# Two transformer layers on one core: transposes at the ends of attention units moved to VectorE in 32x32 blocks, the rotary pair exchange done by a shuffle, and an RMS norm applied behind its products

## The chip, the cores and the metric

The kernel runs on one core of a Trainium2 chip. The metric is the device time of one execution in microseconds (us). The core has five engines that run their own instruction queues in order: PE (TensorE; the profile lists its weight loads apart, as PEld), DVE (VectorE), ACT (ScalarE), POOL (GpSimd) and SP (SyncE, which here only issues DMAs). They wait for each other through semaphores. PE writes its products to PSUM, eight banks of 128 partitions by 512 fp32 numbers; everything else lies in SBUF (128 partitions) or in HBM, the chip's main memory.

## The reference, cut to what matters

The input is 4096 rows of 256 features. Two layers follow each other, both with a layer norm first and a residual sum behind, and all attentions have 16 heads of width 16:

```python
xn = layernorm(x)
x  = x + sparse_attention(xn) + fp8_product(xn)          # layer 0
xn = layernorm(x)
x  = x + rope_attention(xn) + moe_block(xn)              # layer 1

def sparse_attention(x):     # keys: every 8th row, and the query's own block of 128, masked
    q, k, v = split(x @ W + b); return softmax(q k^T / 4 + mask) v @ Wproj + bproj
def rope_attention(x):       # full causal attention
    q, k, v = split(x @ Wqkv)
    rope(t) = t * cos + (-t_odd, t_even interleaved) * sin        # pairs of features
    return softmax(rope(q) rope(k)^T / 4 + causal) v @ Wproj
def moe_block(x):
    h = rms(x) * n1_w        # rms(x) = x * rsqrt(mean(x*x) + EPS)
    q = rms_per_head(h @ wq.T) * qn_w;  k = rms_per_head(h @ wk.T) * kn_w;  v = h @ wv.T
    x = x + softmax(q k^T / 4 + causal) v @ wo.T                   # first 64 columns zeroed
    xf = rms(x) * n2_w
    return x + weighted sum of the best two of four experts(xf)   # first 64 columns zeroed
```

So there are three attentions: a = 0 (sparse), a = 1 (rotary) and a = 2 (inside the MoE block, full causal).

## The kernel before

**Tiling.** Rows are cut into 8 chunks of 512 (CW), each of four tiles of 128 (P); heads into 4 groups of four. One **unit** (`unit`, line 1194) is one attention `a`, one group `g` and one chunk `ch` of queries: 3 x 4 x 8 = 96 units. A causal unit of chunk ch has 4(ch+1) tiles of 128 keys, a sparse one has four tiles of strided keys and the local blocks. I call the work on one such tile of keys a **round**: scores of four heads (`st_a`), their exponentials on ACT (`pt_a`), and the products with the values into one PSUM bank (`po_a`).

**Two passes over the scores.** The softmax subtracts the true maximum. The first pass (`causal_max`, `strided_max`, `local_max`, from line 947) makes scores with queries along the partitions in `pm_a` (`pms_a`, `pml_a`) and DVE reduces each 512-wide bank to a column of `mx_a`. The second pass (`exponentials`, line 1021) makes them again the other way round, adds the negated maximum by a small product with the constant `pick` and the tile `sh_a`, and exponentiates. The first pass of one unit runs interleaved with the second pass of the unit in front, one group of maxima with each half round.

**Between the passes of a unit.** `reduced` (line 990) takes the maximum over a unit's columns (`nm_a`), splits it in a high and a low part, and lays the two in `pad`. `shift` (line 1004) transposes the four tiles of `pad` on PE into a bank (`ps_a`), and ACT copies the bank to `sh_a`, where the 16 rows that are needed lie along the queries.

**At the end of a unit.** `out_copied` (line 1099) copies the sums out of PSUM (`oc_a`), `out_turned` (line 1103) transposes them on PE in four blocks of 128x128 (`pot_a`), `out_divided` (line 1108) copies that bank (`od_a`, ACT), inverts the softmax sums (`rd_a`, DVE), and multiplies (`on_a`, POOL). When the four groups of a chunk are done, two further sets of four PE transposes (`pon`, by `turn`, line 266) turn the result back, ACT copies it (`ot`, `proj_copied`, line 1123), and `projected` and `added` (lines 1128, 1162) make the output projection and the residual sum.

**Preparation.** `prepare0` (line 393) and `prepare1` (line 484) make q, k and v of one chunk for layer 0 and for layer 1 and store them in HBM. In `prepare1`, q and k of the rotary attention are each made twice, with the weights and with the weights whose columns are swapped in pairs (`_swap`, line 1368), so that rope is two multiplications on DVE and one addition on POOL. For the MoE attention the layer-normed rows are multiplied by their RMS factor (`scaled`, line 514: `hr`), transposed once more on PE (`pth`) and scaled by n1_w on the way out (`kept_h`, line 521: `ht`).

**Order.** `Schedule` (line 65) sorts all pieces by a key; one unit of key is about four rounds. A unit starts its second pass at a0 and its first pass at m0 = a0 - lag. `units` (line 1276) sets the lag: at least size + 0.5, where size is ch + 1 for a causal unit and 1.25 for a sparse one. For causal units of chunks 1 to 7 the lag is size + 1; for the first 20 units it is size + 0.5. `between` (line 1282) puts a **block** of preparation and expert work, all at one key, into the gap behind certain units; there are nine. `add_ring` and `add_open` hold back pieces that need a PSUM bank: four banks in the ring "bank" (scores of the second pass, transposes, projections), three in the ring "max" (first pass, experts). The helper `InOrder` (line 42) keeps every engine to the order in which the pieces come; since it records each instruction, nearly all groups of the profile carry its line, L52, and are told apart by tile names.

**Queues.** Almost all DMAs go through SP in that same order: key tiles for both passes (`load_k`, line 862, keys m0 - 1 + i and a0 - 1 + i), values, queries, weights, and the stores. SP waits until a DMA's buffer is free, and everything behind it waits too.

Of the kernel before, what the change touches and what calls it, by code (L numbers as in the profile page):

```python
# [37 lines left out]
RMS_EPS = 1.1920929e-07  # L38
F32_MAX = 3.4028234663852886e38
# [69 lines left out]
def tile_two_layers(ctx: ExitStack, tc, d, out):  # L109
# [44 lines left out]
    y_d = dram.tile([NCH, P, TPC, E], BF16, name="y_d")  # L154
    x1_d, xn_d, s_d, x2_d, xs_d = (
# [6 lines left out]
    with ExitStack() as at:  # L162
# [23 lines left out]
        pads = []  # L186
        for i in range(2):
            pad = c1.tile([P, TPC, 2, 64], F32, name=f"pad{i}")
            nc.gpsimd.memset(pad, 0.0)
            nc.gpsimd.memset(pad[:, :, :, 2 * HPG : 2 * HPG + 1], 1.0)  # L190
            pads.append(pad)
# [109 lines left out]
        def act_piece(todo, fn):  # L301
            todo.append((fn, None, None))
# [49 lines left out]
        def v_products(todo, src, w, a, place, bias, nm):  # L352

            for tp in range(2):
# [11 lines left out]
                def drain(z=z, tp=tp):  # L366
                    v = vst[vst_no[0] % 2]
                    vst_no[0] += 1
                    act.copy(
                        v.rearrange("p t h d -> p (t h) d")[:, :, 0:D], z["p"].rearrange("p t (h d) -> p (t h) d", d=D)  # L370
                    )
# [112 lines left out]
        def prepare1(ch):  # L484
# [4 lines left out]
                [("w1", 2), ("w1", 3), ("w1", 0), ("w1", 1), ("w1", 4), ("w2", 1), ("w2", 2), ("w2", 0)], nm,  # L489
# [17 lines left out]
            def squares():  # L507
                sp.dma_start(xn_d[ch], s["x"])
                s["rr"] = rms(s["x"], nm)
# [4 lines left out]
            def scaled():  # L514
                s["hr"] = work.tile([P, TPC, E], F32, tag="t1", name="hr" + nm)
                for t in range(TPC):
                    dve.tensor_scalar(s["hr"][:, t, :], s["x"][:, t, :], s["rr"][:, t : t + 1], None, ALU.mult)

            act_piece(todo, scaled)

            def kept_h(f, pt):
                if f == 0:
                    s["ht"] = work.tile([P, 2, CW], F32, tag="ht", name="ht" + nm)
                act.activation(s["ht"][:, f, :], pt, AF.Copy, scale=nw1[:, f : f + 1])


            for n, (what, dst) in enumerate((("k", k_d[1]), ("q", q_d[1]))):
# [3 lines left out]
                def part(half, i, n=n, what=what, scale=scale, parts=parts):  # L531
                    z, name = parts[half], f"{what}1{half}"

                    def mm():
                        feature_product(z, w[2 * n + i], s["xt"], half, f"p{name}{i}{nm}")

                    def ev():
                        z[i] = work.tile([P, CW], F32, tag=f"r{i}", name=f"r{i}_{name}{nm}", bufs=2 - i)
                        dve.scalar_tensor_tensor(z[i], z["p"], scale, s["cs"][:, i, :], ALU.mult, ALU.mult)
                        if i:  # L540
                            pool.tensor_tensor(z[0], z[0], z[1], ALU.add)

                    todo.append((mm, "bank", ev))

                for i in range(2):
                    for half in range(2):
                        part(half, i)
                    act_piece(todo, w.fetch)
# [7 lines left out]
                if n == 0:  # L556
                    turn(todo, lambda: s["hr"], kept_h, "pth" + nm)

            v_products(todo, lambda: s["xt"], lambda: w[4], 1, ch, None, nm)


            for what, n, wcol, dst in (("k", 5, 1, k_d[2]), ("q", 7, 0, q_d[2])):
# [13 lines left out]
                def sq2(tp, z=z, name=name):  # L576
                    if tp == 0:
                        z["raw"] = work.tile([P, TPC, E], F32, tag="t1", name=f"raw_{name}{nm}")
                        z["ss"] = small.tile([P, TPC * H], F32, tag="ss2", name=f"ss2_{name}{nm}")
                        z["rs"] = small.tile([P, TPC * H], F32, tag="rs2", name=f"rs2_{name}{nm}")  # L580
                    act.copy(z["raw"][:, 2 * tp : 2 * tp + 2], z[tp])
                    sq = work.tile([P, 2 * E], F32, tag="r1", name=f"sq2_{name}{tp}{nm}")
# [4 lines left out]
                def norms2(z=z, name=name):  # L587

                    x, y = z["ss"], z["rs"]
                    t = small.tile([P, TPC * H], F32, tag="nt2", name=f"nt2_{name}{nm}")  # L590
                    dve.tensor_scalar(x, x, 1.0 / D, RMS_EPS, ALU.mult, ALU.add)
# [30 lines left out]
            v_products(rest, lambda: s["ht"], lambda: w[6], 2, ch, None, nm)  # L622
# [8 lines left out]
        def rms(x, nm):  # L631

            sq = work.tile([P, CW], F32, tag="r1", name="sqj" + nm)[:, :E]
# [3 lines left out]
            ve = small.tile([P, TPC], F32, tag="ve", name="rve" + nm)  # L637
            dve.tensor_scalar(ve, ss, 1.0 / E, RMS_EPS, ALU.mult, ALU.add)
            rs = small.tile([P, TPC], F32, tag="rr", name="rrs" + nm)
            pool.tensor_tensor(rs, ve, mhalf[:, :TPC], ALU.pow)  # L640
            return rs
# [39 lines left out]
        def experts(ch):  # L681
# [7 lines left out]
            def squares():  # L689
                s["rr"] = rms(s["x"], nm)  # L690
# [299 lines left out]
        def reduced(u, n):  # L990

            neg = small.tile([P, TPC * HPG], F32, tag="nm", name="nm_" + u["nm"])
# [3 lines left out]
            pad = pads[unit_no[0] % 2]  # L996
            unit_no[0] += 1
            src = neg.rearrange("p (t h) -> p t h", h=HPG).unsqueeze(2).to_broadcast([P, TPC, 2, HPG])
            high = pad[:, :, :, 0 : 2 * HPG : 2]
            dve.tensor_copy(pad.bitcast(F32R)[:, :, :, 0 : 2 * HPG : 2], src)  # L1000
            dve.tensor_tensor(pad[:, :, :, 1 : 2 * HPG : 2], src, high, ALU.subtract)
            u["pad"] = pad.rearrange("p t i c -> p t (i c)")

        def shift(u):
            ps_ = bank_tile("ps_" + u["nm"])
            for t in range(TPC):
                pe.transpose(ps_[:, tt(t)], u["pad"][:, t], ident)
            u["sh"] = work.tile([P, CW], F32R, tag="sh", name="sh_" + u["nm"], bufs=2)
            act.copy(u["sh"], ps_)
# [87 lines left out]
        ons, proj = {}, {}  # L1097
# [5 lines left out]
        def out_turned(u):  # L1103
            u["pt"] = bank_tile("pot_" + u["nm"])
            for t in range(TPC):
                pe.transpose(u["pt"][:, tt(t)], u["oc"][:, tt(t)], ident)

        def out_divided(u):
            od = work.tile([P, CW], F32, tag="oc", name="od_" + u["nm"], bufs=2)
            act.copy(od, u["pt"])  # L1110
            v = od.rearrange("p (q r) -> p q r", r=R)
            rd = small.tile([P, TPC * HPG], F32, tag="rd", name="rd_" + u["nm"])
            dve.reciprocal(rd, v[:, :, D])
            at_ = u["a"], u["ch"]
            if u["g"] == 0:
                ons[at_] = work.tile([P, TPC, E], F32, tag="on", name=f"on_{u['nm']}", bufs=2)
            on = ons[at_].rearrange("p t (g h d) -> p t g h d", g=G, d=D)[:, :, u["g"]]
            pool.tensor_tensor(
                on, v[:, :, 0:D].rearrange("p (t h) d -> p t h d", h=HPG),
                rd.rearrange("p (t h) -> p t h", h=HPG).unsqueeze(3).to_broadcast([P, TPC, HPG, D]), ALU.mult,  # L1120
            )

        def proj_copied(a, ch, f, pt):
            if f == 0:
                proj["ot"] = work.tile([P, 2, CW], F32, tag="xt", name=f"ot_{a}_{ch}")
            act.copy(proj["ot"][:, f, :], pt)

        def projected(a, ch, tp):
            n = wp[a].shape[2]
            pp = bank_tile(f"pp_{a}_{ch}_{tp}").rearrange("p (t f) -> p t f", t=2)  # L1130
            for j in range(2):
                for c in range(2):
                    pe.matmul(
                        pp[:, j, :n], proj["ot"][:, c, tt(2 * tp + j)], wp[a][:, c, :],
# [59 lines left out]
        def unit(a, g, ch, a0, lag, m0, own_at):  # L1194
# [8 lines left out]
            for kc in keys:  # L1203
                at = tiles.index((kc, 0)) / TPC if a and kc != ch else own_at / TPC if a else keys.index(kc)
                sched.add(m0 - 1.0 + at, load_k, u, kc, "km")
# [279 lines left out]
```

## Time and profile before

| what | value |
|---|---|
| median of 3 runs | 5221.17 us (5215.86 to 5225.06) |
| the profiled execution | 5228.83 us, of which the profile's span is 5227.1 us |
| PE busy | 5021.6 us, 96% of the span |
| DVE busy | 3636.3 us, 70% |
| ACT busy | 3163.8 us, 61% |
| POOL busy | 577.6 us, 11% |
| mean granted TensorE clock | 0.977 of full speed |
| DMA | 737.31 MB, 141 GB/s on average |

The profile's page gives busy times for the whole span. It is read here together with four answers of the trace: groups of instructions with their shapes (number, busy time in us, mean ns of one, idle time in front of them), tables of windows (busy time of each engine in one stretch of time, with the number of instructions in brackets), the timeline, and the list of DMAs with the time from issue to landing. Transposes count one record each on PE; an fp32 product of 128 rows of contraction counts two. The busy time of a group is the union of its records, which overlap, so it is less than number times mean.

### The profile page before, as it was taken

The page shows a single profiled execution, that of the slowest core. Times are in us where ns is not written, and L with a number is a line of the kernel's source. Part 1 is how long each engine was busy: PE and PEld are TensorE (multiplying, and loading weights), DVE is VectorE, ACT ScalarE, POOL GpSimd, SP SyncE. Part 2 cuts the span into 40 slices and gives each one's busy share as a digit, 9 for nine tenths or more (in the row PEclk, how much of TensorE's full clock was granted, in tenths as well). Part 3 has the DMA queues.
Part 4 walks back from the last instruction along what each step waited for, and adds up shares of the span by engine and source line. Part 5 has one row for each costly group of instructions (what it writes and reads, how often), then busy time and mean ns, then how long its engine had stood idle before and what let it go on. Part 6 is the DMA issues. An engine that isn't in the chain of part 4 may idle for free.

```text
span 5227.1 us, 98240 instructions
## 1 busy us (share of the span) xinstructions
PE 5021.6 (96%) x35680; PEld 2674.8 (51%) x35680; DVE 3636.3 (70%) x8215; ACT 3163.8 (61%) x6351; POOL 577.6 (11%) x557
## 2 busy tenths in 40 slices
PE   6788899999999999999999999999999999999999
PEld 3455555555655555554545454545445544444445
DVE  4655774777488838888387886588885698888701
ACT  2544573576367736777376775567774567777752
POOL 3232113111201020100301001001001000000000
PEclk7889899999999999999999999999999999999999
DMA  5465545444634444433544334434334433333222
GB/s 192 148 209 183 172 150 184 157 158 136 203 119 152 142 153 158 149 123 130 172 144 145 121 120 140 154 118 140 119 106 146 152 113 127 113 118 119 98 76 80
DMA packets 497458, 737.31 MB, mean 141 GB/s; under 512 B 97104, under 2 KB 203088, under 8 KB 496976
## 3 DMA queue, kind: packets, MB, share of 16 engines
q1 hardware_dynamic: 492576, 728.58, 42.1%
q8 instruction: 285, 4.67, 0.4%
q10 hardware_dynamic: 4400, 2.45, 0.2%
q14 instruction: 197, 1.61, 0.1%
HBM read 586.90 MB, written 143.95 MB: 140 GB/s over the span
## 4 chain that ended last, share of the span: by engine, by line
PE 84%; DVE 7%; issue 4%; POOL 2%; DMA 1%; ACT 1%; SPq 0%; ACTq 0%; POOLq 0%; DVEq 0%
PE st_a L52 27%; PE po_a L52 22%; PE pm_a L52 12%; DVE pms_a L52 2%; PE pe_m L52 2%; PE pk L52 2%; PE pq L52 2%; PE pp L52 2%; DVE mx_a L52 1%; PE pml_a L52 1%; PE pv L52 1%; PE pms_a L52 1%; PE ps_a L52 1%; PE pot_a L52 1%; POOL x L52 1%
## 5 line engine op out<-in xcount | busy, mean ns | idle before, releaser
L52 ACT ACTIVATE pt_a<-st_a 128x512 f32<-128x512 f32 (+3 forms) x5248 | 2599.9, 572 | 1056.6 <-PE st_a L52 1002.7
L52 DVE TENSOR_REDUCE mx_a<-pm_a 128x1 f32<-128x512 f32 x3584 | 2232.0, 683 | 301.1 <-PE pm_a L52 225.8
L52 PE MATMUL pm_a<-km_a,q_a 64*128 64x512 f32 (+3 forms) x4608 | 1840.4, 434 | 21.3 <-DVE mx_a L52 18.4
L52 PE MATMUL st_a<-q_a,ke_a 64*128 64x512 f32 (+3 forms) x5632 | 1777.3, 401 | 1.7 <-ACT pt_a L52 1.6
L52 PE MATMUL st_a<-sh_a,pick_r 64*128 64x512 f32 (+3 forms) x5248 | 1729.5, 398 | 0.0
L52 PEld LDWEIGHTS st_a<-q_a,ke_a 64*128 64x128 f32 x5632 | 899.6, 187 | 1022.2 <-ACT pt_a L52 919.4
L52 PE MATMUL po_a<-pt_a,v 128*32 128x512 f32 (+3 forms) x11264 | 1325.0, 549 | 0.0
L52 PEld LDWEIGHTS pm_a<-km_a,q_a 64*128 64x128 f32 x4608 | 843.2, 185 | 360.2 <-DVE mx_a L52 313.4
L52 PEld LDWEIGHTS st_a<-sh_a,pick_r 64*128 64x128 f32 x5248 | 951.5, 187 | 44.0 <-issue 2.9
L52 DVE CUSTOM_DVE_ANT_0 pm_a<-pm_a,never_sb 128x512 f32<-128x512 f32 (+3 forms) x1024 | 482.2, 515 | 182.3 <-PE st_a L52 97.0
L52 DVE CUSTOM_DVE_ANT_0 pms_a<-pms_a,hidden_sb 128x512 f32<-128x512 f32 x512 | 341.0, 719 | 85.0 <-PE pms_a L52 77.2
L52 POOL TENSOR_TENSOR on_a<-od_a,rd_a 128x256 f32<-128x256 f32 x96 | 59.6, 621 | 3064.1 <-DVE rd_a L52 3064.1
L52 PEld LDWEIGHTS po_a<-pt_a,v 128*32 128x32 f32 x11264 | 228.6, 108 | 306.8 <-issue 273.6
L52 PE MATMUL pms_a<-km_a,q_a 64*128 64x512 f32 x512 | 224.3, 509 | 33.4 <-DVE mx_a L52 18.5
L52 PE MATMUL st_a<-mcol_sb,identb_sb 64*128 64x128 bf16 x2048 | 255.2, 224 | 0.0
L52 DVE SCALAR_TENSOR_TENSOR acc_m<-pe_m,g_wt_m,acc_m 128x192 f32<-128x192 f32 x128 | 52.6, 416 | 268.9 <-PE pe_m L52 268.9
L52 DVE DVE_READ_ACCUMULATOR2_ANT mx_a<- 128x1 f32 x1536 | 217.8, 142 | 0.0
L52 PEld LDWEIGHTS pms_a<-km_a,q_a 64*128 64x128 f32 x512 | 95.7, 195 | 67.1 <-DVE mx_a L52 49.8
L52 PEld LDWEIGHTS <-identb_sb 64*128 64x128 bf16 x2048 | 114.0, 96 | 12.0 <-issue 4.1
L52 ACT CAST sh_a<-ps_a 128x512 fp32r<-128x512 f32 x96 | 56.2, 586 | 91.9 <-PE ps_a L52 91.9
L52 DVE TENSOR_REDUCE mx_a<-pml_a 128x4 f32<-128x512 f32 x128 | 83.1, 688 | 25.5 <-PE pml_a L52 25.3
L52 POOL TENSOR_TENSOR xa<-xa,pa 128x512 f32<-128x512 f32 (+1 forms) x48 | 56.9, 1185 | 357.4 <-ACT pa L52 350.6
(401 smaller groups left out, 4167.4 us busy)
## 6 DMA issues: line engine op xcount, KB each, us to landing
km_a<-k_d SPq DMA_DIRECT2D x704, 256.0 KB, 4.1
ke_a<-k_d SPq DMA_DIRECT2D x704, 256.0 KB, 3.1
k_d<-hl_k SPq DMA_DIRECT2D x100, 512.0 KB, 3.3
q_d<-hl_q SPq DMA_DIRECT2D x96, 512.0 KB, 4.8
q_a<-q_d SPq DMA_DIRECT2D x192, 256.0 KB, 4.6
v<-v_d SPq DMA_DIRECT2D x352, 136.0 KB, 4.0
w<-in_w_dram SPq DMA_DIRECT2D x85, 256.0 KB, 4.7
w_l<-in_l_dram SPq DMA_DIRECT2D x80, 256.0 KB, 2.9
```

The costliest lines, as they stand in the source:

```text
L52: got = emit(*args, **kw)
```

## The change

1. **The maxima.** `reduced` packs the high and low parts into 32 columns, transposes them on DVE in 32x32 blocks (`turned`, tile `tu`), and SP writes the blocks with four DMAs to a new tensor `shift_d` in HBM. `shift` is now two DMAs on SP that read the unit's 8 rows back, twice, into one of two standing tiles (`rows_`) whose row of ones was laid out at the start. PE transposes `ps_a` and the ACT copy are gone. Both steps get new keys: a0 - lag + size + 0.05 and + 0.1 (before: a0 - min(0.8, lag - size - 0.05), and a0 - min(0.3, lag - size - 0.3)).
2. **The outputs.** `out_turned` is gone; `out_divided` transposes `oc` on DVE (512 columns, 32x32 blocks), inverts on DVE and multiplies on POOL into a tile `om` that two groups share; behind every second group `out_returned` transposes `om` back on DVE into `ot`. The four `pon` sets and their ACT copies are gone. The rows of the projection weights are reordered on the host to suit (`_by_turns`).
3. **Rope.** The products with swapped weights are gone. ACT copies the product out of PSUM, DVE exchanges neighbours by a stream shuffle, POOL multiplies by sin, DVE multiplies by cos, POOL adds.
4. **The MoE norm.** `hr` and `pth` are gone: `ht` is `xt` times n1_w, made on ACT. The RMS factor is applied where v leaves PSUM (two ACT instructions of 256 columns in place of one of 512), and for q and k it is folded into the EPS term of the norm per head (`norms2`: one small DVE instruction more).
5. **Smaller.** The load of a sparse unit's own keys for the first pass goes from key m0 to m0 + 0.4. Some tiles change tags and buffer counts.

```diff
-            pad = pads[unit_no[0] % 2]
+            pad = small.tile([P, TPC, HPG, 2], F32, tag="pad", name="pad_" + u["nm"])
+            src = neg.rearrange("p (t h) -> p t h", h=HPG)
+            high = pad[:, :, :, 0]
+            dve.tensor_copy(pad.bitcast(F32R)[:, :, :, 0], src)
+            dve.tensor_tensor(pad.bitcast(F32R)[:, :, :, 1], src, high, ALU.subtract)
+            turned = small.tile([P, R], F32, tag="tu", name="tu_" + u["nm"])
+            dve.transpose(turned, pad.rearrange("p t h i -> p (t h i)"))
+            no = unit_no[0]
             unit_no[0] += 1
...
+            rows = shift_d[no].rearrange("r (t b j) -> b t r j", t=TPC, b=TPC)
+            for b in range(TPC):
+                sp.dma_start(rows[b], turned[R * b : R * (b + 1), :])
+            u["no"], u["sh"] = no, rows_[no % 2]

         def shift(u):
-            ps_ = bank_tile("ps_" + u["nm"])
-            for t in range(TPC):
-                pe.transpose(ps_[:, tt(t)], u["pad"][:, t], ident)
-            u["sh"] = work.tile([P, CW], F32R, tag="sh", name="sh_" + u["nm"], bufs=2)
-            act.copy(u["sh"], ps_)
+            for half in (0, 64):
+                sp.dma_start(u["sh"].bitcast(F32)[half : half + 2 * HPG, :], shift_d[u["no"]])
...
         def out_divided(u):
             od = work.tile([P, CW], F32, tag="oc", name="od_" + u["nm"], bufs=2)
-            act.copy(od, u["pt"])
+            dve.transpose(od, u["oc"])
...
+        def out_returned(u):
...
+            dve.transpose(proj["ot", at_][:, f, :], outs.pop(at_))
...
                     def ev():
-                        z[i] = work.tile([P, CW], F32, tag=f"r{i}", name=f"r{i}_{name}{nm}", bufs=2 - i)
-                        dve.scalar_tensor_tensor(z[i], z["p"], scale, s["cs"][:, i, :], ALU.mult, ALU.mult)
-                        if i:
-                            pool.tensor_tensor(z[0], z[0], z[1], ALU.add)
+                        z[0] = work.tile([P, CW], F32, tag="r0", name=f"r0_{name}{nm}", bufs=2)
+                        act.activation(z[0], z["p"], AF.Copy, scale=scale)
+
+                    def rotated():
+                        z[1] = work.tile([P, CW], F32, tag="r1", name=f"r1_{name}{nm}", bufs=2)
+                        dve.stream_shuffle(z[1], z[0], PAIRS)
+                        pool.tensor_tensor(z[1], z[1], s["cs"][:, 1, :], ALU.mult)
+                        dve.tensor_tensor(z[0], z[0], s["cs"][:, 0, :], ALU.mult)
+                        pool.tensor_tensor(z[0], z[0], z[1], ALU.add)
...
-            sched.add(a0 - min(0.8, lag - size - 0.05), reduced, u, len(keys))
-            sched.add_ring(a0 - min(0.3, lag - size - 0.3), "bank", 1, shift, u)
+            sched.add(a0 - lag + size + 0.05, reduced, u, len(keys))
+            sched.add(a0 - lag + size + 0.1, shift, u)
...
-            put(e0 + 0.12, lambda: out_turned(u), "bank", lambda: out_divided(u))
+            sched.add(e0 + 0.05, out_divided, u)
+            if g % 2:
+                sched.add(e0 + 0.35, out_returned, u)
             if g == G - 1:
-                turns = []
-                turn(turns, lambda: ons[a, ch], lambda f, pt: proj_copied(a, ch, f, pt), f"pon_{a}_{ch}")
-                for f in range(2):
-                    put(e0 + 0.5 + 0.13 * f, *turns[f])
```

## The prediction

> **What bounds the kernel now.** I read the page first: busy times and the chain of waits.
>
> ```profile
> PE 5021.6 (96%) x35680; PEld 2674.8 (51%) x35680; DVE 3636.3 (70%) x8215; ACT 3163.8 (61%) x6351; POOL 577.6 (11%) x557
> ...
> PE 84%; DVE 7%; issue 4%; POOL 2%; DMA 1%; ACT 1%; SPq 0%; ACTq 0%; POOLq 0%; DVEq 0%
> ```
>
> PE looks like the only bound, and the change takes PE work away. The groups by shape give its size (busy us, mean ns of one):
>
> ```profile
> L52 PE MATMUL pk<-xt,w 128*128 128x512 f32 x184 | 91.7, 628 | 2.3 <-ACT xt L52 2.3
> L52 PE MATMUL pq<-xt,w 128*128 128x512 f32 x184 | 85.3, 593 | 0.0
> ...
> L52 PE MATMUL ps_a<-ident_sb,pad 128*128 128x128 f32 x384 | 64.8, 293 | 2.1 <-DVE pad L52 2.1
> ...
> L52 PE MATMUL pot_a<-ident_sb,oc_a 128*128 128x128 f32 x384 | 63.0, 287 | 0.0
> ...
> L52 PE MATMUL pon<-ident_sb,on_a 128*128 128x128 f32 x192 | 31.2, 285 | 1.0 <-ACT pt_a L52 0.8
> ...
> L52 PE MATMUL pth<-ident_sb,hr 128*128 128x128 f32 x64 | 10.2, 283 | 0.0
> ```
>
> Rope's second products are 2 halves x 2 contractions x 2 records = 8 records of pk and 8 of pq per chunk, 64 of each in all: 64 x 91.7/184 + 64 x 85.3/184 = 61.6 us. With the four transposes PE loses 64.8 + 63.0 + 31.2 + 10.2 + 61.6 = 230.8 us. But an average over the span hides what else is full, so I cut single rounds out of a unit of chunk 5 (windows; PE, PEld, DVE, ACT, POOL busy):
>
> ```profile
> 3416.69:3419.45 2.76, 2.76 (x46) 1.87 (x45) 2.49 (x5) 2.65 (x6) 0.00 (x0) 1.00 0.56 195
> 3419.45:3422.83 3.38, 3.38 (x27) 1.56 (x25) 2.60 (x5) 2.71 (x7) 0.00 (x0) 1.00 0.00 0
> 3422.83:3425.57 2.74, 2.74 (x23) 1.23 (x21) 2.57 (x5) 1.93 (x5) 0.62 (x1) 1.00 0.00 1
> 3425.57:3428.30 2.73, 2.73 (x23) 1.21 (x21) 2.48 (x5) 2.07 (x5) 0.00 (x0) 1.00 0.82 267
> ```
>
> The last row is a plain full round: 2.73 us, in which DVE's four reductions take 2.48. DVE is 91% busy here, not 70%. The second row holds `pot`: 0.65 us longer. The third holds the reciprocal (0.25 us of DVE) and is no longer: it fits in DVE's 0.25 us of idle time. The timeline shows why nothing more would fit. In each round PE waits about 0.3 us for DVE to free a bank of the first pass, with three such banks for pairs of products. So **PE and DVE are locked together**, and DVE work above 0.25 us in a round delays PE by the excess.
>
> **Part 1, preparation blocks.** Per chunk go 7.5 us of rope products (16 records at some 0.47 us, the pace inside these windows) and 1.2 us of `pth`. Two of the blocks:
>
> ```profile
> 252.00:343.00 91.00, 59.99 (x238) 38.42 (x228) 42.76 (x100) 28.61 (x56) 43.44 (x37) 0.79 0.56 184
> ...
> 1833.00:1978.00 145.00, 140.25 (x528) 85.93 (x528) 55.10 (x138) 48.50 (x89) 43.90 (x37) 0.98 0.52 170
> ```
>
> The second has an expert body and PE is full (97%); six chunks are prepared in such blocks: 6 x 8.7 = 52 us gained. DVE and POOL have room there for a shuffle, a multiplication (taken at the 0.69 us of the `r_k` row, against two of these removed) and one more POOL multiplication of 1.27 us (row `r_k<-r_k,r_k`). In the first kind PE is busy 60 of 91 us and waits 15.4 us for `raw_q` from DVE; with POOL at 43 us and 5 us more, I count 6 us for those two blocks (bounds -10 and +17). `norms2` gets a DVE instruction of 0.19 us on the path PE waits for, 16 times: 3 us lost. **Sum: 55 us gained.**
>
> **Part 2, transposes on DVE.** No row shows a DVE transpose. Nearest is the reduction of 128x512 (0.62 us from start to start, 0.68 for one): below, it can't be cheaper than about 0.6, as it passes the same 512 elements. Above, fp32 might go at half or a quarter of that pace: 1.2 or 2.3 us. [...] For 32 columns I take the 0.19 us of `pad`.
>
> In a full round with `pot`, the new time is the larger of PE's and DVE's: 3.38 - 0.65 = 2.73, against 2.48 + 0.69 + 0.25 = 3.42. **So moving the output transpose gains nothing there**: its 0.65 us come back as 0.68. The transpose back (every second unit) adds 2.48 + 0.69 - 2.73 = 0.44 in the next round. I made this comparison for every round outside the blocks, with its own length and DVE time. `ps` sits in rounds on the diagonal, whose score products are narrower, and gives nearly all its 0.65: -64 us with those that also hold `pon`. The 32-column transpose costs +9, the output transposes +2 (gains in chunk 0 and at the end, losses elsewhere), `pon` against the way back 0. **Sum: 53 us gained of 154 removed**; at 0.62 us it would be 61, at 1.2 us a loss of 11, at 2.3 us a loss of 155.
>
> [...] With DVE simply full, each added instruction would cost its whole time: 96 x (0.19 + 0.69) + 48 x 0.69 = 118 us against 154, a gain of 36. The rows give more, as a round has 0.25 us free and not all rounds are full.
>
> ACT loses the `sh`, `od` and `ot` copies (56 + 57 + 29 us) and gains 32 of 0.6. It is never the last here; I count nothing.
>
> **Part 3, the maxima through HBM.** This is a new wait. Before, in the timeline of an early unit (start, length, engine):
>
> ```profile
> 568.99 0.19 DVE L52 TENSOR_REDUCE nm_a<-mx_a 128x16 f32<-128x32 f32 x1
> ...
> 570.88 0.66 PE L52 MATMUL ps_a<-ident_sb,pad 128*128 128x128 f32 x4
> ...
> 571.57 0.58 ACT L52 CAST sh_a<-ps_a 128x512 fp32r<-128x512 f32 x1 [0.57 <-PE ps_a L52]
> ...
> 573.87 0.50 PE L52 MATMUL st_a<-q_a,ke_a 64*128 64x512 f32 x1
> ```
>
> From `nm_a` to the first product that needs it PE has 5 us here. Now: DVE 0.75, four issues on SP, a landing, two issues, a landing. The nearest rows (KB, us to landing):
>
> ```profile
> y_d<-y SPq DMA_DIRECT2D x16, 128.0 KB, 1.7
> ya<-y_d SPq DMA_DIRECT2D x16, 128.0 KB, 3.1
> ```
>
> An issue takes 0.33 us there; small reads land in 2.5 at best. 0.75 + 4 x 0.37 + 1.5 + 0.1 + 0.4 + 2.5 + 0.1 = 6.8 us; with landings at the slow end of those rows (4.0 and 5.3 us) 11.9. What it has:
> - 76 units with a wide lag: 7.5 us or more in the trace (4510.2 to 4517.7 in chunk 7), plus 2.9 since `reduced` moves one diagonal round forward, less the 0.65 of `ps`: 9.7 us. Hidden, with 2.9 to spare.
> - The first 20 units keep their key: 4.1 to 8.9 us, less 0.65. Three reach across a block. Unit by unit the shortfalls against 6.8 sum to 11 us.
>
> Queued behind these DMAs on SP are the key, value and query loads of later keys. They are issued a whole unit of key ahead (about 11 us) and land in 3 to 4 us, so being held for 5 us is covered, but only just. In front of them early on stand the stores of `added`, which wait for POOL, and SP's backlog after a block: 9 us more. **Sum: 20 us lost** (0 to 75 for the first units alone).
>
> **The sum.** -55 - 53 + 20 = -88 us: 5228.8 - 88 = 5141 for an execution like the profiled one. The median shown lies 7.7 us below that execution: **5133 us**, 1.7% faster.
>
> **The rivals.**
> - *The whole PE gain.* The 96% and the 84% of the chain speak for it, the 2.48 of 2.73 us against it. 5221 - 231 = 4990; PE regaining most of it, under 5080.
> - *Slower transposes, about 1.2 us.* Part 2 becomes +11: 5221 - 55 + 11 + 20 = 5197; near 1.4 us all is gone. Nothing in the trace speaks for or against it.
> - *Quarter-pace transposes, 2.3 us:* slower, 5221 - 55 + 155 + 20 = 5341; it decides from 1.4 us on.
> - *The way through HBM becomes the bound (slower).* Place: PE's first score product of each unit waits for the two reads. Price at 11 us: 70 wide units x 1.3 + 17 early ones x 4.4 = 166 us in place of 20: 5279. It decides from about 10.3 us. For it: SP waits in order, landings reach 5 us. Against it: DMA is under half busy, the transfers are small.
>
> **How the numbers follow.** Forecast (5080 to 5185) 0.48; whole PE gain 0.16; 1.2 us transposes 0.10; 2.3 us 0.09; HBM way 0.17. Faster, same and slower are told apart at 0.2%, about what the three runs' spread lets one see. Of the 1.2 us case most is "same": faster 0.66, same 0.08, slower 0.26. The range 5050 to 5260 leaves out the best of the PE case and the worst half of the slower ones. The forecast's own range is 5080 to 5185.
>
> **What would show it.** A DVE row for `od_a` of about 0.69 us; full rounds still 2.73 us, those with `od_a` about 3.4; expert blocks of 136 us instead of 145; no PE wait for DMAs into the maxima's rows from chunk 1 on, some in the first 650 us. Plain rounds shorter than 2.7 us would prove my coupling of PE and DVE wrong; a PE wait in every unit would prove the HBM rival.

## The result, and the profile after

The changed kernel takes 5239.59 us (median of 15 runs, 5221.94 to 5249.18), the kernel before 5223.02 us (15 runs, 5215.67 to 5243.99): ratio 1.0027, 95% interval 1.0015 to 1.0038. It is **slower by 0.27%** where 1.7% faster was forecast. The time lies inside the range on record, on the wrong side of no change.

The page of the changed kernel, the lines on busy time and on the chain of waits:

```profile
PE 4900.2 (94%) x34528; PEld 2561.5 (49%) x34528; DVE 3750.0 (72%) x8473; ACT 3066.6 (59%) x6159; POOL 621.9 (12%) x587
...
PE 17%; issue 3%; DVE 2%; POOL 0%; ACT 0%; POOLq 0%; ACTq 0%
```

PE has lost 121 us of busy time, not the 231 us of the removed products. Part of the difference can be the granted clock: its mean is 0.963 against 0.977 before, which over the span makes up to 72 us. The chain breaks off early this time, so its shares add up to little and say nothing; the reading has to come from stages and waits. DVE's new rows (groups by shape; busy us, mean ns of one, idle time in front and what ended it):

```profile
L53 DVE STREAM_TRANSPOSE od_a<-oc_a 128x512 f32<-128x512 f32 x96 | 67.3, 701 | 10.0 <-ACT oc_a L53 10.0
L53 DVE STREAM_TRANSPOSE ot_a<-om_a 128x512 f32<-128x512 f32 x48 | 33.8, 704 | 18.9 <-POOL om_a L53 18.9
...
L53 DVE TENSOR_TENSOR r_q<-r_q,cs 128x512 f32<-128x512 f32 x16 | 27.5, 1717 | 1.7
...
L53 DVE TENSOR_TENSOR r_k<-r_k,cs 128x512 f32<-128x512 f32 x16 | 11.9, 744 | 0.5
```

The transposes take 0.70 us, the prediction's 0.69: both rivals with slow transposes are out. But the second row has something that was not forecast: DVE stands 18.9 us before `ot_a`, waiting for POOL. And the same multiplication takes 0.74 us on average in one place and 1.72 us in another.

Next, single rounds at the end of a unit of chunk 7 (windows; PE, PEld, DVE, ACT, POOL busy, then granted clock, DMA share, GB/s). First the kernel before: its five last rounds, on the diagonal, with the reduction `nm_a` in the second and `ps_a` in the fourth, and, after a gap, the round with `pot_a`.

```profile
4506.08:4509.04 2.96, 2.96 (x30) 1.78 (x29) 2.71 (x8) 2.04 (x5) 0.00 (x0) 1.00 0.85 278
4509.04:4511.88 2.84, 2.84 (x30) 1.61 (x28) 2.77 (x13) 2.12 (x6) 0.00 (x0) 1.00 0.38 134
4511.88:4514.19 2.31, 2.31 (x30) 1.33 (x29) 1.99 (x11) 1.29 (x5) 0.00 (x0) 1.00 0.00 0
4514.19:4516.79 2.60, 2.60 (x33) 1.71 (x32) 1.62 (x11) 1.63 (x6) 0.00 (x0) 1.00 0.00 0
4516.79:4519.11 2.32, 2.32 (x23) 1.21 (x21) 1.63 (x6) 1.37 (x4) 0.00 (x0) 1.00 0.81 249
4521.49:4524.86 3.37, 3.37 (x26) 1.56 (x24) 2.60 (x5) 2.76 (x7) 0.00 (x0) 1.00 0.04 11
```

Then the changed kernel: a plain full round, the same five rounds, and, after a gap, the rounds with `od_a` and with `ot_a`.

```profile
4519.57:4522.31 2.74, 2.74 (x22) 1.20 (x20) 2.47 (x5) 2.06 (x5) 0.00 (x0) 1.00 0.00 0
4522.31:4525.73 3.42, 3.27 (x30) 1.73 (x28) 3.28 (x10) 2.50 (x6) 0.00 (x0) 1.00 0.00 0
4525.73:4528.33 2.60, 2.60 (x29) 1.61 (x28) 2.56 (x11) 1.51 (x4) 0.00 (x0) 1.00 0.09 15
4528.33:4530.64 2.31, 2.31 (x31) 1.34 (x29) 1.93 (x10) 1.52 (x6) 0.00 (x0) 1.00 0.38 99
4530.64:4532.49 1.85, 1.85 (x29) 1.15 (x28) 1.46 (x10) 1.04 (x5) 0.00 (x0) 1.00 0.92 332
4532.49:4534.80 2.31, 2.31 (x24) 1.21 (x21) 1.67 (x7) 1.39 (x5) 0.00 (x0) 1.00 1.02 344
4537.19:4540.44 3.25, 2.87 (x23) 1.21 (x21) 3.22 (x7) 2.64 (x6) 0.62 (x1) 1.00 0.09 28
4540.44:4543.42 2.98, 2.86 (x23) 1.20 (x21) 2.98 (x6) 1.91 (x5) 0.00 (x0) 1.00 0.06 11
```

A plain round is unchanged: 2.74 us, although much PE work is gone from the kernel. The reduction has moved into the first of the five rounds, where DVE is full (3.28 of 3.42 us). That round grows by 0.46 us, the next shrinks by 0.24, and the fourth gives back 0.75. The five together go from 13.03 to 12.49 us. With `od_a` a round takes 3.25 us, where `pot_a` made 3.37; with `ot_a` it takes 2.98.

To find where such gains went I set the ends of all 96 units side by side (the start of ACT's copy `oc_a`) and summed the differences by what a unit follows. All figures are us of the profiled executions; e1, e2 and e3 are the experiments below, each adding one part.

| units | before to after | before to e1 | e1 to e2 | e2 to e3 | after to e3 |
|---|---|---|---|---|---|
| first 20, no block in front (17) | +15.4 | +15.8 | -5.8 | -1.4 | -6.9 |
| first 20, behind a block (3) | +17.7 | +2.6 | +16.0 | +2.3 | +3.3 |
| later, behind a block (6) | -28.6 | +15.4 | -48.7 | +2.7 | -2.1 |
| later, sparse (20) | -17.9 | +2.2 | -0.5 | -20.3 | -0.6 |
| later, causal behind a sparse one (21) | +32.8 | +7.8 | -3.3 | -6.0 | -34.3 |
| later, causal behind a causal one (29) | -7.8 | -7.1 | +2.6 | -9.8 | -6.5 |
| all | +11.6 | +36.7 | -39.7 | -32.5 | -47.1 |

Expert blocks and sparse units gain, the six blocks 4.8 us each where 8.7 were forecast. The first 20 units, and causal units that follow a sparse one, lose it all again. One such unit (a = 1, g = 0, chunk 3) shows a new wait. Its timeline in the changed kernel (start, length, engine; idle time in front in brackets):

```profile
1604.32 1.27 POOL L53 TENSOR_TENSOR xs<-xs,xa 128x512 f32<-128x512 f32 x1 [2.57 <-DMA xs<-s_d]
1605.54 0.62 POOL L53 TENSOR_TENSOR om_a<-od_a,rd_a 128x256 f32<-128x256 f32 x1
...
1606.19 0.71 DVE L53 STREAM_TRANSPOSE ot_a<-om_a 128x512 f32<-128x512 f32 x1 [2.73 <-POOL om_a L53]
...
1607.53 0.28 PEld L53 LDWEIGHTS pm_a<-km_a,q_a 64*128 64x128 f32 x1 [3.39 <-DVE mx_a L53]
```

POOL waits for a load (`xs`, for the residual sums of another unit), its multiplication `om_a` waits behind it, DVE stands at `ot_a` and makes no maxima, and PE's weight load waits 3.39 us for those, its product 2.95. Three engines in a row stand for one DMA that only POOL's sum needs.

The chain of waits comes six times, in the first unit (g = 0) of the rotary attention of chunks 1 to 6. These six waits are the 18.9 us of DVE, and PE's products stand 2.95 to 4.03 us each time. And each is followed by a second loss. The windows of the same place have the granted clock in the column before the last two:

```profile
1602.00:1606.30 4.30, 2.58 (x20) 1.02 (x18) 1.57 (x4) 2.67 (x6) 1.99 (x3) 1.00 0.63 213
1606.30:1613.10 6.80, 5.56 (x26) 2.42 (x30) 4.96 (x9) 2.06 (x4) 2.24 (x2) 0.50 0.82 266
```

Still within the wait the clock falls to half, for 6.8 us. At all six it does so, from within the wait or at most 1 us behind it, for 3.4 or 6.8 us; that is 34 us together, in which 17 us of full clock are lost.

PE's waits in the whole changed kernel:

```profile
PE pm_a L53 <- DVE mx_a L53: 86.5, 131, 4.2
...
PE st_a L53 <- DMA rows<-shift_d: 14.7, 9, 5.1
...
PE pml_a L53 <- DMA km_a<-k_d: 8.6, 8, 2.0
```

The wait for the maxima's way through HBM is 14.7 us, nine times, all in the first 690 us. The wait for DVE's maxima is the large one (18.4 us before). The last row, a wait for keys, is new.

### The profile page after: what moved, and what is told of

The parts are those of the page before. It is cut to its first block, busy times and chain, and to the rows that moved or that the text cites. A ratio compares the mean times of both kernels' runs of the same rounds, so it can differ in the third digit from the quotient of the medians.

```text
span 5238.4 us, 96849 instructions
## 1 busy us (share of the span) xinstructions
PE 4900.2 (94%) x34528; PEld 2561.5 (49%) x34528; DVE 3750.0 (72%) x8473; ACT 3066.6 (59%) x6159; POOL 621.9 (12%) x587
## 5 line engine op out<-in xcount | busy, mean ns | idle before, releaser
L53 PE MATMUL st_a<-rows,pick_r 64*128 64x512 f32 (+3 forms) x5248 | 1759.8, 404 | 14.7 <-DMA rows<-shift_d 14.7
L53 PEld LDWEIGHTS st_a<-q_a,ke_a 64*128 64x128 f32 x5632 | 911.5, 188 | 1032.1 <-ACT pt_a L53 938.2
L53 PE MATMUL po_a<-pt_a,v 128*32 128x512 f32 (+3 forms) x11264 | 1339.7, 554 | 0.0
L53 PEld LDWEIGHTS st_a<-rows,pick_r 64*128 64x128 f32 x5248 | 957.0, 188 | 75.0 <-DMA rows<-shift_d 19.4
L53 POOL TENSOR_TENSOR om_a<-od_a,rd_a 128x256 f32<-128x256 f32 x96 | 59.7, 622 | 3053.7 <-DVE rd_a L53 2928.1
L53 PE MATMUL pt<-ident_sb,x 128*128 128x128 f32 x136 | 35.5, 361 | 62.3 <-POOL x L53 62.3
```

The source lines that it names most:

```text
L53: got = emit(*args, **kw)
```

## The experiments

Ratios are to the kernel before, run on the same chip; times are medians. The edits that are not parts of the change put together are given as short diffs.

### The parts, one after the other

**e1** has the maxima's part alone. **e2** adds rope and the norm. **e3** is the changed kernel, thus all parts, with one key moved:

```diff
             if g % 2:
-                sched.add(e0 + 0.35, out_returned, u)
+                sched.add(e0 + 0.75, out_returned, u)
```

> The kernel before with only the way of the maxima through HBM (new keys and the later load of the sparse units' own keys included). The prediction's terms: -64 for ps, +9 for the 32-column transpose, +20 for waits, so -35 us: about 5188. New theory, from the trace after: the reduction now stands in full rounds and lengthens some 64 of them by 0.6 us (+38), the early units and the late key load cost some 25 more, ps gives its 60 back: about 0 to +15, 5223 to 5238.

> The run above plus rope by shuffle and the MoE norm behind its products. The prediction's term is -55 us against the run above. New theory: six expert blocks give 4 us each instead of 8.7, and the first two blocks lose 6 to 10 us each because POOL, not PE, carries them: -10 to -15 us against the run above.

> The changed kernel with one key moved: out_returned from e0 + 0.35 to e0 + 0.75. Theory: DVE stands before ot_a for POOL's om_a, which stands behind a stream load on POOL, and PE then waits for DVE's maxima; 18.9 us of DVE waits go, and PE's time with them: -15 to -20 us, about 5220. Rival: PE would have lost that time elsewhere (DVE is full in these rounds), so less than 5 us.

Measured: e1 5263.28 us (1.0066, 1.0053 to 1.0078), e2 5235.87 (1.0016, 1.0007 to 1.0024), e3 5202.70 (0.9949, 0.9936 to 0.9963).

- The maxima's part alone costs 34.6 us. That is more even than the new theory had, and the opposite of the prediction's -35.
- Rope and norm gain 27 us by the medians. The six later blocks give 48.7 us by the profiled executions (8.1 each, forecast 8.7, so my new theory of 4 each was wrong: the maxima's part had cost these blocks 15.4 us in e1; against the kernel before, e5 below has them 7.7 us shorter each), the first three lose 16, nearly all of it in the second and the third. The profiled execution of e2 lies below its median, so the table's -39.7 is somewhat too good.
- Moving `out_returned` by 0.4 of a key gains 0.78% (1.0027 against 0.9949), some 41 us and twice what I expected. The table's last column has it where the timeline showed it: -34.3 of -47.1 us behind sparse units (the profiled execution of e3 is its fastest, so the table is again somewhat too good). In e3 the row of `ot_a` shows no idle time in front of it. At the place above POOL still waits for the load, but DVE no longer for POOL:

```profile
1587.22 1.29 POOL L53 TENSOR_TENSOR xs<-xs,xa 128x512 f32<-128x512 f32 x1 [2.44 <-DMA xs<-s_d]
1588.46 0.63 POOL L53 TENSOR_TENSOR om_a<-od_a,rd_a 128x256 f32<-128x256 f32 x1
...
1591.91 0.70 DVE L53 STREAM_TRANSPOSE ot_a<-om_a 128x512 f32<-128x512 f32 x1
```

The six units take 339.1 us in e3 and 373.6 in the changed kernel: all of the gain behind sparse units lies in them. The six waits of PE (20 us) and the six stretches at half clock (17 us) are gone, which is the size of it. So the chain of waits at `ot_a`, with the clock that falls behind it, is **shown** as the cause of that loss, and I expected half because I counted the waits alone. Taken from e2, the output transposes placed thus gain 0.67%, 35 us.

### What the maxima's way costs, and why

**e9** is the kernel before with the new key of `reduced` alone. **e10** adds six DMAs per unit on SP, which wait for the reduction as the change's do, but which nothing needs (one `pad` tile serves all units, to make room). **e12** adds the later load of a sparse unit's own keys.

The edit of all three, then that of e10 and e12, then that of e12:

```diff
-            sched.add(a0 - min(0.8, lag - size - 0.05), reduced, u, len(keys))
+            sched.add(a0 - lag + size + 0.05, reduced, u, len(keys))
```

```diff
+            for b in range(TPC):
+                sp.dma_start(side_d[no, R * b : R * (b + 1)], neg[R * b : R * (b + 1), :])
+            back = side_d[no].rearrange("(r a) c -> r (a c)", r=8)
+            for half in (0, 64):
+                sp.dma_start(side[half : half + 2 * HPG, :], back)
```

```diff
-                sched.add(m0 - 1.0 + at, load_k, u, kc, "km")
+                sched.add(m0 - (1.0 if a or kc == NCH else 0.6) + at, load_k, u, kc, "km")
```

**e13** is e3 with that load put back for chunks 3 to 7:

```diff
-                sched.add(m0 - (1.0 if a or kc == NCH else 0.6) + at, load_k, u, kc, "km")
+                sched.add(m0 - (1.0 if a or kc == NCH or ch > 2 else 0.6) + at, load_k, u, kc, "km")
```

> The kernel before with one key changed: reduced at the change's key (a0 - lag + size + 0.05), the PE transposes left at theirs. Theory (DVE full): the reduction of 76 wide units moves from a diagonal into a full round, which grows by 0.6 us, while the diagonal round gives about 0.35 back: +15 to +25 us, 5240 to 5252. Rival: the full round has room for it, within 5 us of before.

> The run above, plus for each unit four stores of nm to HBM and two reads of them back, all on SP, whose result nothing uses: no PE product waits for them, and DVE does nothing more. One pad tile serves all units, to find room. Theory (SP held): +30 to +45 us against the run above, as SP stands before the stores and the loads behind start late. Rival (length of the way): only the wait of PE for rows costs, so within 5 us of the run above.

> The run with SP held alone (5249), plus the change's later key for the load of a sparse unit's own keys (m0 + 0.4), which puts that load behind the stores in SP's order. Theory (order on SP): the hold was covered only while these loads stood in front of it: +10 to +20 us, with PE waits for km_a of some 9 us. Rival: the later load is covered too, within 5 us of 5249; then the rest of the cost is in the strided stores' longer issue (0.62 us against 0.43) and in PE's own wait for rows.

> The changed kernel with out_returned at e0 + 0.75 (5203), and with the own-key load of the sparse units of chunks 3 to 7 back at m0, in front of the stores. Theory (order on SP): -8 to -20 us, and the 8.7 us of PE waits for km_a gone. Rival: the load now is in front, but the stores and all behind them come later: within 5 us of 5203, or slower.

Measured: e9 5249.04 us (1.0036, 1.0022 to 1.0050), e10 5248.67 (1.0044, 1.0032 to 1.0056), e12 5271.55 (1.0087, 1.0073 to 1.0101), e13 5180.81 (0.9909, 0.9893 to 0.9925).

e9: the key costs 0.36%, 19 us (11 to 26). The size was as expected, the place was not: in the chunk 7 unit above the five rounds take 13.05 us in e9 against 13.03, and of the 18.1 us by which e9's profiled execution is behind at the end of the last unit, 10.5 come in sparse units.

e10: a miss. SP stands 482.6 us in the whole before the stores and 149.7 before the reads, and it costs nothing that can be measured. e12 is the answer: one load put behind the stores makes it 0.43%, 22 us. e13 confirms it from the other side: 0.40%, 21 us gained, one microsecond past what I expected. So the hold is free up to a margin, and the change goes over it.

Where the price is paid differs between the two. SP's order at the end of the unit in front of an expert block, in e10 (the unit ends at 1843.65):

```profile
1832.93 1.71 SPq L52 DMA_DIRECT2D side_d<-nm_a  x4
...
1837.78 0.90 SPq L52 DMA_DIRECT2D km_a<-k_d  x2
1838.73 0.43 SPq L52 DMA_DIRECT2D x<-x_d  x1
```

and in e12 (the unit ends at 1857.92):

```profile
1847.20 1.71 SPq L52 DMA_DIRECT2D side_d<-nm_a  x4
...
1851.95 1.85 SPq L52 DMA_DIRECT2D km_a<-k_d  x4
1853.84 0.43 SPq L52 DMA_DIRECT2D x<-x_d  x1
```

In e10 two of the key loads went out ahead of the stores; in e12 all four stand behind, and the load `x`, which the block starts with, is issued 4.1 us before the unit's end in place of 4.9. It lands too late: DVE waits 1.4 us for it in e12, not at all in e10. In e1, with the strided stores' longer issue (2.50 us for four against 1.71), it goes out 2.6 us before the end and DVE waits 2.9. PE's own waits for `km_a` were not the price in e12, as I had expected: 2.2 us besides the one that is in every kernel. But the block is not all of it. Between the profiled executions of e10 (its fastest) and e12 (its slowest) lie 31.5 us, of which 9.5 come in the six blocks and 13.1 in causal units behind sparse ones. There the stretches at half clock cost 13.6 us more, and in the 10 us in front of the two longest PE shows no wait of 0.2 us; so how far this share is e12's doing is not settled.

In e13 it is the keys. The changed kernel and e3 have PE waits for the sparse units' own keys, 8.6 and 8.7 us (`pml_a` for `km_a`), which e13 no longer has, as expected, and 15.5 of the 19.7 us between the profiled executions of e3 and e13 come in the causal units behind sparse ones, where these waits stand. The six blocks gain 1.4 us, although DVE's waits for `x` there fall from 17.0 to 9.6 us.

### Another place and another queue

**e4** is the changed kernel with `reduced` back at its old key and the reads right behind. **e7** is e3 with the six DMAs on POOL's queue (`pool.dma_start` in place of `sp.dma_start` in `reduced` and `shift`). **e8** is e7 with the old keys of `reduced` and of the key load, and the reads right behind the reduction. **e11** is e7 for units 20 to 79 only:

```diff
-                sp.dma_start(rows[b], turned[R * b : R * (b + 1), :])
+                (pool if 20 <= no < 80 else sp).dma_start(rows[b], turned[R * b : R * (b + 1), :])
```

> The changed kernel with the old key of reduced (a0 - 0.8, in a diagonal round) and the two reads right behind it. Theory: 64 full rounds lose their 0.6 us and the diagonal round takes the reduction for nothing: -30 to -40 us, about 5200 to 5210, if the way through HBM (about 6.5 us) still fits into the 7 us left. Rival (HBM way): it does not fit, PE waits for rows in most units, and the time stays at 5240 or rises.

> The changed kernel with out_returned at e0 + 0.75 and the six DMAs of each unit's maxima issued by POOL in place of SP. Theory (SP held): what the HBM way costs is that SP stands before the stores of the maxima until DVE has made them, so that the loads behind them start late; on POOL's queue nothing of that kind stands behind: -25 to -35 us against the same kernel on SP (5203), about 5172. Rival (DVE full): the cost is the reduction in full rounds, which stays: within 8 us of 5203.

> As the run above, with the reduction back at a0 - 0.8, the reads right behind it and the sparse units' own keys loaded at m0 as before. SP is then free of the wait, so only the length of the way counts. Theory: about 6.5 us fit into the 7 to 9 us, and the full rounds lose 0.6 us 64 times: 20 to 35 us less than the run above. Rival: the way does not fit, PE waits for rows in most units (over 60 us in sum), and the time is above the run above.

> The changed kernel with out_returned at e0 + 0.75, and the six DMAs issued by POOL only for units 20 to 79 in order of reduction (the late chunk 1 to chunk 5), by SP for the others. Theory (SP held): the 33 us that POOL's queue gave between units 26 and 75, without the 80 us that it cost in the first 20 units: 5165 to 5180. Rival: the gain was only the early units' lag made up: within 8 us of 5203.

Measured: e4 5330.14 us (1.0195, 1.0181 to 1.0210), e7 5256.35 (1.0060, 1.0047 to 1.0073), e8 5366.38 (1.0272, 1.0256 to 1.0287), e11 5162.67 (0.9878, 0.9865 to 0.9892).

The old place of the reduction is far too late for the way through HBM. On SP's queue (e4) it is not PE's wait for `rows` that grows but that for keys, whose loads stand behind:

```profile
PE pml_a L53 <- DMA km_a<-k_d: 33.3, 10, 4.3
...
PE pm_a L53 <- DMA km_a<-k_d: 20.4, 19, 2.0
PE st_a L53 <- DMA rows<-shift_d: 18.5, 11, 5.4
```

On POOL's (e8) the keys are in time, and PE waits for `rows`:

```profile
PE st_a L53 <- DMA rows<-shift_d: 147.3, 64, 10.1
```

So this rival of mine was right in e8 and right about e4's time, though not about its wait.

e7 looks like a failure of the theory, but unit by unit it is two things. Up to unit 26 it loses 84 us against e3: the way is longer behind POOL's own work and its waits, and the first 20 units have no time to spare (PE waits 81.5 us for `rows` in the whole, in e3 16.5). From there to unit 75 (chunk 5, behind its block) it gains 33 us, the forecast's size. e11 keeps only that stretch and gains 0.71%, 37 us, against e3. Taking the DMAs off the queue that carries the loads is worth that much; what issues them in their place must have nothing behind it that is urgent, and time.

### Versions that put the parts where they fit

**e5** is the kernel before with rope, norm and output transposes (`out_returned` at e0 + 0.75), and with the maxima's old way; to make room it has one `pad` tile and fewer buffers for rope. **e6** is e5 with one line changed (below). **e14** mixes the two ways of the maxima by unit number (the old way for the first 20, POOL's queue to 79, SP's after), with the line of e6 and the later `out_returned`.

```diff
-                        pool.tensor_tensor(z[1], z[1], s["cs"][:, 1, :], ALU.mult)
+                        dve.tensor_tensor(z[1], z[1], s["cs"][:, 1, :], ALU.mult)
```

> The kernel before with rope, the norm and the output transposes of the change, out_returned at e0 + 0.75, and the maxima's old way (PE transposes and ACT copy, old keys). To find room one pad tile serves all units, and the second half's shuffle result lies in the tile pa. Theory: the parts add up, -27 to -40 from the blocks and -33 from the outputs, none of the 35 us of the HBM way: 5155 to 5170. Rival: without the space that the removal of ps gave, DVE's output transposes cost their full time, so 5190 or more.

> As the run above, with the multiplication by sin on DVE in place of POOL. Theory: in the two blocks without experts POOL carries the work, and four multiplications of 1.27 us per chunk leave it: 8 to 12 us less than the run above, and the row r_q<-r_q,cs of DVE falls from 1.7 us to 0.7. Rival: the block's length is set elsewhere: no difference above 3 us.

> Each way where it is cheap: the first 20 units with the maxima's old way (PE transposes into the standing rows, old keys), units 20 to 79 through HBM on POOL's queue, the others on SP's; out_returned at e0 + 0.75, both rope multiplications on DVE, the other parts as in the change. From the unit-by-unit comparison of the runs: 5163 of the run with POOL's queue in the middle, less 17 for the early units, less 5 for rope: 5135 to 5148. Rival: the gains do not add up, since DVE is the bound in the early units: 5155 or more.

Measured: e5 5161.84 us (0.9877, 0.9864 to 0.9891), e6 5156.58 (0.9868, 0.9852 to 0.9883), e14 5145.71 (0.9847, 0.9834 to 0.9861).

The parts add up. e14 is 1.5% faster than the kernel before and 1.8% faster than the changed one. But e6, with the maxima's old way in all units, is 1.3% faster too, and the two intervals overlap: that the way through HBM gains anything, even where it fits, is not shown. e13's key is not in e14; the two were not tried together. e6 shows why one multiplication took 1.7 us: with POOL's multiplication gone, its row falls to half, first e5, then e6:

```profile
L53 DVE TENSOR_TENSOR r_q<-r_q,cs 128x512 f32<-128x512 f32 x16 | 27.4, 1714 | 1.7
```

```profile
L53 DVE TENSOR_TENSOR r_q<-r_q,cs 128x512 f32<-128x512 f32 x32 | 23.9, 787 | 0.5
```

DVE makes twice as many in less time. The whole kernel gains only some 5 us (the intervals overlap), half of what I expected. By the profiled executions the first three blocks, 14.8 us longer in e5 than before, get back 3.2: POOL's multiplication is the smaller part of what they lose.

## Why the prediction was wrong

The forecast was -88 us; the medians show +16.6, by the ratio +14. Term by term, with what the runs showed (ratios turned into us):

| term | forecast | shown | by |
|---|---|---|---|
| blocks (rope, norm) | -55 | -26 | e1 to e2 |
| output transposes themselves | +2 | -35 | e2 to e3 |
| where `out_returned` stands | 0 | +41 | e3 to after |
| maxima: `ps` gone, transpose in, way through HBM | -64 + 9 + 20 = -35 | +34 | before to e1 |
| sum | -88 | +14 | |

**The step that failed first** is "the transpose back (every second unit) adds 2.48 + 0.69 - 2.73 = 0.44 in the next round". It priced a DVE instruction by its own length and did not ask what it waits for. `om_a` comes from POOL, and POOL's queue holds `added` with its loads. The prediction did ask that question for SP (the stores of `added`), not for DVE, where the answer cost 41 us: six waits, and the half clock behind each.

**The second** is "issued a whole unit of key ahead ... so being held for 5 us is covered, but only just". e10 shows that the hold alone was covered, e12 and e13 that with the key load behind it the hold is not: 21 to 22 us. The smaller part of the change, the load at m0 + 0.4, was listed and got no price. The loads that came late were the sparse units' own keys (PE waits 8.6 us for them in the changed kernel) and the rows `x` of the next block (DVE waits 15.2 us for them there; before, it never does), which the prediction did not look at.

**The third** is the -64 us for `ps`. In a chunk 7 unit the section on the diagonal gives 0.54 us, near the forecast; but over the 29 causal units behind causal ones e1 gains only 7.1 us, 0.25 each, and the sparse ones lose 2.2. The key of `reduced` alone costs 19 us (e9). The prediction took that move as extra time for the transfer and charged DVE with the transpose of 0.19 us alone, while the whole reduction went to another round with it. What remains of the difference (69 us less 19, less 22, some 28) is not split further by the runs: the strided stores' longer issue and the smaller gain from `ps` are in it, and the clock, whose stretches at half cost 31 us more in e1's profiled execution than before, 20 of them in the first 700 us.

What was right: the coupling of PE and DVE. Plain rounds stayed at 2.74 us, and the 0.65 us of PE work taken from the round with `pot` came back almost whole as DVE's (3.25 us for 3.37). That is why the rival of the whole PE gain is dead. The 0.69 us per transpose in the sums of part 2 was my estimate, which no row of the kernel before shows (the nearest is a reduction's 0.68); the changed kernel showed 0.70 (701 and 704 ns). The rounds were priced a little too high: `od_a` makes 3.25 us, not 3.42, and `ot_a` 2.98, not the 3.17 that 2.73 + 0.44 gives. Against 3.37 with `pot`, and with the `pon` sets gone, that is where my +2 turned to a gain; but 20.3 of the table's 32.5 us lie in sparse units, whose rounds I did not cut out, so the 35 us are not worked out in full. The expert blocks gave 8.1 us each against 8.7. The first blocks lost 16 us, near the far end of the bound named (+17). My reason, that POOL carries them, explains only the 3 us that e6 gave back; in e2 the stretches at half clock cost 13.6 us more there than before. A slip without weight: the slow end of the way through HBM adds up to 12.1 us, not 11.9.

**The rival that won** is the slower one, the way through HBM, but not by its mechanism. It had PE's first score product wait for the reads in each unit; PE waits for `rows` nine times, all early, 14.7 us in the whole, as the main forecast said. What costs is what stands behind these DMAs on SP. And the wait that decided between faster and slower, at `ot_a`, was in none of my cases: e3 alone, with everything else as in the change, is 0.5% faster than the kernel before.

A term that the prediction did not have is the granted clock. Its stretches at half take away 191 us of full clock in the changed kernel's profiled execution and 119 before; only the 17 us at `ot_a` are traced to their waits, by e3. In the first 20 units they take 36 us more, about what these units lose in all (33.1). Left open: which of the waits there bring them, and the share of `weighted`, for which PE waits 11.4 us in two blocks.

## What to carry to other kernels

Price a moved instruction by what it waits for and by what stands behind it on its engine, not by its length: here 0.7 us of work on DVE cost PE 3 to 4 us six times, and a stretch at half clock each time, because its input came from a third queue that was waiting for a load. A queue that issues loads ahead of time can lose its lead to an entry that waits for present work: here 21 to 22 us with the sparse units' key load behind it (e12, e13), nothing that can be measured without that (e10). Count how much lead the latest of the loads behind needs, also those of the next stage. And where one kernel has stages with different margins, choose the way by stage: POOL's queue in all units made e3 1.1% slower, in the 60 units with time to spare 0.7% faster. And measure the old way beside the mixture: e6, which keeps it in all units, comes within the noise of e14.

## What the runs showed of the hardware

- In the changed kernel a transpose of 128x512 fp32 in 32x32 blocks on DVE took 701 ns, about as long as a reduction of that size (681 ns); a stream shuffle took 722 ns.
- Where DVE and POOL each multiplied a 128x512 fp32 tile by `cs` at nearly the same time in the changed kernel, the one that began second took longer. Four times POOL began 0.05 us behind DVE and took 1.78 us, DVE 0.69; 14 times DVE began 0.02 to 0.03 us behind POOL and took 1.79, POOL 1.27. First one with DVE ahead, then one with POOL ahead:

```profile
3254.50 0.69 DVE L53 TENSOR_TENSOR r_k<-r_k,cs 128x512 f32<-128x512 f32 x1
3254.55 1.78 POOL L53 TENSOR_TENSOR r_k<-r_k,cs 128x512 f32<-128x512 f32 x1 [5.56 <-DVE r_k L53]
...
3270.44 1.27 POOL L53 TENSOR_TENSOR r_q<-r_q,cs 128x512 f32<-128x512 f32 x1 [3.47 <-DVE r_q L53]
...
3270.46 1.79 DVE L53 TENSOR_TENSOR r_q<-r_q,cs 128x512 f32<-128x512 f32 x1
```

e6 agrees: with both multiplications on DVE the row has 0.79 us a piece, in e5 1.71. It was not so beside every instruction of POOL: beside its scaling of `x` (TENSOR_SCALAR, which reads one tile) the same multiplication of DVE kept its 0.69 us, at 274.16 us. I had priced this instruction at 0.69 us and had not looked at who runs beside it.
- SP took 0.62 us to issue one of the change's strided stores of 4 KB (2.50 us for four, in e1), 0.43 us for a plain one of 2 KB (1.71 us for four, in e10) and 0.45 us for a key load of 256 KB (0.90 us for two, in e10): here the price on the issuing queue did not follow the bytes.
- The granted clock fell to 0.50 for 3.4 or 6.8 us at each of the six waits of 2.95 to 4.03 us at `ot_a`, and did not at those places in e3. It also fell to 0.50 at 4251.66 us of the changed kernel, for 3.4 us, where PE shows no wait of 0.2 us in the 10 us in front, so these waits are not its only cause.
